# Graph product of a two-layer graph network: three pairs in seven block products, with h's blocks and sums kept in DRAM

## The chip, the cores and the metric

The kernel runs on one core of a Trainium2 chip. The metric is the device time of one execution in microseconds (us); the median of several runs is compared. All data is 32-bit float.

## The reference

For 16 batches of 1024 nodes with 256 channels there are two layers, each adding its result to x.

```python
# layer 0
h = relu(layernorm(x))
fea = h.transpose(0, 2, 1)                    # b, c, n
c = mean(fea, axis=1)                         # b, n: mean over the channels
A = abs(abs(sigmoid(c[:, None, :] - c[:, :, None]) - 0.5) - 0.5) * 2
g = relu(einsum('bcn,bnm->bcm', fea, adj * (A + A^T) / 2) * para)
q = g^T in 4 heads of 64;  k, v = h @ kv_w in 4 heads
x = x + softmax(q k^T * scale) v
# layer 1
h = relu(layernorm(x))
z = relu(batchnorm((A_hat h) @ W1.T + b1))    # A_hat: normalised adj + I, batchnorm over all rows
x = x + batchnorm(z @ W2.T + b2)
```

The change is in `einsum('bcn,bnm->bcm')`, here called the graph product: for each batch the transposed h (256 x 1024) times a weight matrix (1024 x 1024) that depends on the batch.

## The kernel before

The 1024 nodes of a batch are cut into NC = 8 blocks of 128 rows. The loop over b (lines 1306 onwards) does attention of batch b, then the graph product, values and keys of batch b+1, then the first linear stage of layer 1 for batch b (linear1_all). Batch 1 uses graph(), the later ones, 2 to 15, graph_seven(): 14 calls. After the loop, W2 and the batch norms follow; the change doesn't touch them.

Everything inside runs under a manual schedule: each engine (PE, ACT, DVE, POOL and SP, which issues transfers) executes its instructions in the order in which the program text issues them. Where a line stands decides what it queues behind on its own engine.

A weight block c (tile f_w, 128 x 1024) is made in two parts. `differences(b, c)` is two activations on ACT (lines 350 and 353), reading the row of sums f_row and writing the block. `masked(b, c)` is one instruction on DVE (line 358), which multiplies the block by the adjacency rows. The blocks live in the pool w4, which has five buffers; blocks 0 and 1 are made within the attention before.

In graph_seven the first PLAIN = 4 blocks are multiplied in the ordinary way: `plain(c)` issues 4 products of 128 x 128 by 128 x 512 (line 474). The other four blocks form two pairs. A pair is a 2 x 2 by 2 x 2 block product, and is done with seven products in place of eight (m1 to m_7, line 556), at the price of sums of blocks: t1 to t4 of the weights (lines 522 to 534, half-width subtractions on DVE) and s1 to s4 of h (lines 506 to 509). Three of the seven products add up in one PSUM bank x, from which ACT copies the partial results at three points (lines 589, 599, 604); m6 may write on only when the copy before it is done.

```python
            m1(0)
            m2(0)
            m1(1)
            nc.scalar.copy(room[:, 0], x)
            m_7(0)
```

`turn_h(b)` (line 362) puts h in transposed form into hT: two transposes of 32 x 32 blocks on DVE (line 369) into f_hQ, and 32 transfers on POOL's queue (line 376) from there into f_hT, both in SBUF. hT is wanted by `values` (line 447) and by the keys (line 636). Batch 0 does this on SP's queue.

`left` holds what remains of the attention: add0, collect (ACT), invert (four small DVE instructions, lines 762 to 765), spread (ACT, line 771), scale (DVE, line 780, and 16 transfers on SP's queue, line 797) and add1. graph_seven weaves these in. `partial` in the attention uses f_sums (lines 713 and 721); sums_h takes the same buffer afterwards.

linear1 calls three hooks, between[0] to between[2]. For batch b they prepare h of batch b+2: prepare_start (statistics), prepare_end (ReLU on ACT, line 279), and in linear1_seven prepare_row, which stores h's sums into frow (line 308) and loads them as f_row (line 309), both on SP's queue. linear1_seven makes its own sums on DVE (lines 987 to 991) and its products in line 995; line 1050 adds two of them. `load_thirds` loads six tiles of 512 KB (line 860) just ahead of graph_seven. These, hT and the attention's f_p share the eight buffers with the tag "p"; "acc" has two buffers.

Of the kernel before, what the change touches and what calls it, by code (L numbers as in the profile page):

```python
# [10 lines left out]
F32 = mybir.dt.float32  # L11
# [18 lines left out]
def fast_path(  # L30
# [143 lines left out]
    with ExitStack() as stage:  # L174
# [170 lines left out]
            differences(b, c)  # L345
            masked(b, c)

        def differences(b, c):
            w = w4.tile([P, N], F32, tag="w4", name=f"f_w_{b}_{c}")
            nc.scalar.activation(  # L350
                w, rows[b], AF.Abs, bias=cols[b][:, c : c + 1], scale=0.5 / C
            )
            nc.scalar.activation(w, w, AF.Tanh)  # L353
            ws[b, c] = w

        def masked(b, c):
            w = ws[b, c]
            nc.vector.scalar_tensor_tensor(w, w, 1.0, adj_t[c], ALU.subtract, ALU.mult)  # L358
# [3 lines left out]
        def turn_h(b, queue=nc.gpsimd):  # L362

            hTs[b] = []
            for d in range(CC):
                t = pp.tile([P, 4, NC, 32], F32, tag="acc", name=f"f_hQ_{b}_{d}", bufs=2)
                nc.vector.transpose(
                    t.rearrange("p k c r -> p c k r"),  # L370
                    hs[b][:, :, ts(d, P)].rearrange("p c (k i) -> p c k i", k=4),
                )
# [83 lines left out]
                )  # L456
            return copies

        PLAIN = 4

        def graph_seven(b, left, norm, last):

# [16 lines left out]
                            stop=(c == PLAIN - 1),  # L479
                        )  # L480

            turn_h(b)
            differences(b, 2)
            masked(b, 2)
            collect()
            invert()
            differences(b, 3)
            masked(b, 3)
            differences(b, 4)

            qT = big.tile([P, CC, N], F32, tag="qT", name=f"f_qT_{b}")
            nc.sync.dma_start(qT, para_v)
            spread()
            scale()
            masked(b, 4)
            plain(0)
            differences(b, 5)
            masked(b, 5)
# [3 lines left out]
            pairs_h = h[:, PLAIN:NC, :].rearrange("p (n k) c -> p n k c", k=2)  # L502
            a = lambda i, k: pairs_h[:, :, k, ts(i, P)]
            sums_h = ow.tile([P, 4, 2, P], F32, tag="sums", name=f"f_gs_{b}")
            s1, s2, s3, s4 = (sums_h[:, n] for n in range(4))
            nc.vector.tensor_sub(s3, a(0, 0), a(1, 0))
            nc.vector.tensor_add(s1, a(1, 0), a(1, 1))
            nc.vector.tensor_sub(s2, s1, a(0, 0))
            nc.vector.tensor_sub(s4, a(0, 1), s2)
            plain(1)  # L510
            differences(b, 6)
            masked(b, 6)

            def part_w(n, k, j):
                return ws[b, PLAIN + 2 * n + k][:, ts(j, 512)]

            t2 = [kT[:, n, 0:512] for n in range(2)]
            t3 = [kT[:, n, 512:N] for n in range(2)]
            t1, t4 = [None] * 2, [None] * 2

            def make_t3(n):
                nc.vector.tensor_sub(t3[n], part_w(n, 1, 1), part_w(n, 0, 1))

            def make_t1(n):
                t1[n] = part_w(n, 0, 1)
                nc.vector.tensor_sub(t1[n], t1[n], part_w(n, 0, 0))

            def make_t2(n):
                nc.vector.tensor_sub(t2[n], part_w(n, 1, 1), t1[n])
# [3 lines left out]
                t4[n] = part_w(n, 1, 0)  # L533
                nc.vector.tensor_sub(t4[n], t4[n], t2[n])

            make_t3(0)
            make_t1(0)
            plain(2)
            differences(b, 7)
            masked(b, 7)  # L540
            make_t2(0)
            plain(3)
            hT = hTs.pop(b)
            t23 = pp.tile([P, 2, 512], F32, tag="acc", name=f"f_kt23_{b}", bufs=2)
            rest = pp.tile([P, 2, 512], F32, tag="acc", name=f"f_kt4_{b}", bufs=2)
            sums = rest[:, 1].rearrange("p (n q) -> p n q", n=4)
            nc.sync.dma_start(sums, kvs_d)
            make_t3(1)
            make_t1(1)
            make_t2(1)  # L550
# [4 lines left out]
            def one(ps, left, right, n, more=True, fresh=False):  # L555
                nc.tensor.matmul(  # L556
                    ps,
                    left[:, n, :],
                    right,
                    start=fresh and n == 0,  # L560
                    stop=(n == 1),
                    skip_group_check=more,
                )

            def m1(n):
                one(x, a(0, 0), part_w(n, 0, 0), n, False, True)

            def m2(n):
                one(c_of[0, 0], a(0, 1), part_w(n, 1, 0), n)

            def m3(n):
                one(c_of[0, 1], s4, part_w(n, 1, 1), n)

            def m4(n):
                one(c_of[1, 0], a(1, 1), t4[n], n)

            def m5(n):
                one(x, s1, t1[n], n)

            def m6(n):  # L580
                one(x, s2, t2[n], n)

            def m_7(n):
                one(m7, s3, t3[n], n, False, True)

            m1(0)
            m2(0)
            m1(1)
            nc.scalar.copy(room[:, 0], x)
            m_7(0)  # L590
            m3(0)
            m2(1)
            make_t4(0)
            make_t4(1)
            m6(0)
            m_7(1)
            m3(1)
            m6(1)
            nc.scalar.copy(room[:, 2], x)
            m4(0)  # L600
            m4(1)
            m5(0)
            m5(1)
# [489 lines left out]
        def linear1_all(b, h1, thirds, early, late, last, ending=lambda: None, made=None):  # L1093
# [138 lines left out]
        with tc.manual_schedule(engines={ENG.PE, ENG.Activation, ENG.DVE, ENG.Pool, ENG.SP}):  # L1232
# [73 lines left out]
            for b in range(B):  # L1306
# [34 lines left out]
                    between[3].insert(0, roots_row)  # L1341
                    between[4] = scale[:3] + between[4] + [scale[3]]
                if b + 1 < B:
                    if 0 < b < B - 2:
                        thirds = load_thirds(b)
                    if b == 0:
                        qkv = graph(b + 1, between)
                        todo = []
                    else:
                        qkv, todo = graph_seven(b + 1, left, norm, b + 2 == B)  # L1350
                    if b == 0:
                        for step in scale[4:]:
                            step()
                        thirds = make_thirds(b)
                if b + 2 < B:
# [943 lines left out]
```

## Time and profile before

| | |
|---|---|
| median of 3 runs | 2403.58 us (2402.74 to 2403.99) |
| the profiled execution | 2403.7 us, of which the span is 2401.8 us |
| granted TensorE clock | 0.995 of full speed over the span |
| busy: PE, DVE, ACT, POOL | 98%, 80%, 56%, 13% of the span |
| plain graph products (line 474) | 448 records, 196.0 us together |
| weights: differences, masking | 147.0 and 134.3 us on ACT, 152.8 us on DVE, 127 blocks |
| hT transfers on POOL (line 376) | 480, 500 ns each |

PE is TensorE's matmuls, PEld its weight loads, DVE VectorE, ACT ScalarE, POOL GpSimd, SP the engine that issues most transfers; SPq is its queue. Busy time is the sum of an engine's instructions. One product in the source is two matmul records in the trace. In a line of a timeline the columns are start, length, engine, line of the kernel, operation, output <- input, shape and count; a bracket at the end gives the idle time before the instruction and what ended it.

### The profile page before, as it was taken

The page shows a single profiled execution, that of the slowest core. Times are in us where ns is not written, and L with a number is a line of the kernel's source. Part 1 is how long each engine was busy: PE and PEld are TensorE (multiplying, and loading weights), DVE is VectorE, ACT ScalarE, POOL GpSimd, SP SyncE. Part 2 cuts the span into 40 slices and gives each one's busy share as a digit, 9 for nine tenths or more (in the row PEclk, how much of TensorE's full clock was granted, in tenths as well). Part 3 has the DMA queues.
Part 4 walks back from the last instruction along what each step waited for, and adds up shares of the span by engine and source line. Part 5 has one row for each costly group of instructions (what it writes and reads, how often), then busy time and mean ns, then how long its engine had stood idle before and what let it go on. Part 6 is the DMA issues. An engine that isn't in the chain of part 4 may idle for free.

```text
span 2401.8 us, 24818 instructions
## 1 busy us (share of the span) xinstructions
PE 2364.5 (98%) x7978; PEld 1040.9 (43%) x7978; DVE 1920.9 (80%) x2694; ACT 1346.9 (56%) x1974; POOL 314.7 (13%) x561
## 2 busy tenths in 40 slices
PE   8999999999999999999999999999999999999996
PEld 4443444434343434444343434344443434444445
DVE  6787979696979788797969697887969698757766
ACT  6846555564646455555646465555556465446654
POOL 2030202011020302020210203020202011000000
PEclk9999999999999999999999999999999999999998
DMA  5042423332332414233323324142333122355579
GB/s 188 7 143 62 128 88 110 102 100 68 102 104 68 148 62 135 80 110 105 100 63 107 107 62 146 62 147 69 110 106 107 63 82 65 105 199 189 176 240 379
DMA packets 176411, 275.78 MB, mean 115 GB/s; under 512 B 37648, under 2 KB 121104, under 8 KB 176272
## 3 DMA queue, kind: packets, MB, share of 16 engines
q1 hardware_dynamic: 156112, 241.55, 31.3%
q0 software_dynamic: 15552, 15.77, 2.5%
q10 hardware_dynamic: 4608, 16.78, 1.7%
q8 instruction: 66, 1.08, 0.2%
q14 instruction: 73, 0.60, 0.1%
HBM read 169.35 MB, written 71.10 MB: 100 GB/s over the span
## 4 chain that ended last, share of the span: by engine, by line
PE 97%; DMA 1%; DVE 1%; issue 0%; ACT 0%; SPq 0%; DVEq 0%; ACTq 0%; POOLq 0%; POOL 0%
PE f_s L688 19%; PE f_o L729 19%; PE f_aps L889 16%; PE f_gps L474 8%; PE f_zps L995 6%; PE f_vps L447 4%; PE f_gps L556 4%; PE f_zx L1516 4%; PE f_zm L1516 3%; PE f_gpsx L556 3%; PE f_kpsx L636 2%; PE f_gps L401 2%; PE f_kps L636 1%; PE f_z2ps L1454 1%; PE f_outps L1739 1%; PE f_zps L1077 1%
## 5 line engine op out<-in xcount | busy, mean ns | idle before, releaser
L696 ACT ACTIVATE f_p<-f_s 128x1024 f32<-128x1024 f32 x512 | 477.3, 1046 | 149.1 <-PE f_s L688 149.1
L705 DVE TENSOR_TENSOR f_acc<-f_acc,f_p 128x1024 f32<-128x1024 f32 x384 | 470.5, 1225 | 41.8 <-DVE f_acc L705 1.4
L688 PE MATMUL f_s<-f_qT,f_kT 64*128 64x512 f32 x2048 | 457.1, 596 | 0.0
L729 PE MATMUL f_o<-f_p,f_v 128*64 128x512 f32 x2048 | 453.6, 595 | 0.0
L376 POOL DMA_DIRECT2D f_hT<-f_hQ x480 | 236.7, 500 | 1237.0 <-PE f_gps L474 1161.0
L688 PEld LDWEIGHTS f_s<-f_qT,f_kT 64*128 64x128 f32 x2048 | 190.3, 185 | 264.3 <-ACT f_p L696 118.4
L729 PEld LDWEIGHTS f_o<-f_p,f_v 128*64 128x64 f32 x2048 | 141.3, 137 | 304.4 <-issue 257.0
L474 PE MATMUL f_gps<-f_w,f_h_a 128*128 128x512 f32 x448 | 196.0, 595 | 0.0
L350 ACT ACTIVATE f_w<-f_row,f_col 128x1024 f32<-128x1024 f32 x127 | 147.0, 1158 | 29.6 <-DMA f_row<-frow 26.9
L358 DVE SCALAR_TENSOR_TENSOR f_w<-f_w,f_adj 128x1024 f32<-128x1024 f32 x127 | 152.8, 1213 | 3.8 <-ACT f_w L353 3.8
L353 ACT ACTIVATE f_w<-f_w 128x1024 f32<-128x1024 f32 x127 | 134.3, 1058 | 4.0
L474 PEld LDWEIGHTS f_gps<-f_w,f_h_a 128*128 128x128 f32 x448 | 84.0, 190 | 111.8 <-issue 99.1
L889 PE MATMUL f_aps<-f_ahatT,f_hs 128*128 128x512 f32 x256 | 115.1, 592 | 0.0
L889 PE MATMUL f_aps<-f_ahatT,f_h_b 128*128 128x512 f32 x256 | 113.4, 596 | 0.0
L447 PE MATMUL f_vps<-f_kvw,f_hT 128*128 128x256 f32 x512 | 113.1, 379 | 0.0
L889 PE MATMUL f_aps<-f_t,f_hs 128*128 128x512 f32 x256 | 112.5, 592 | 0.0
L279 ACT ACTIVATE f_h_b<-f_x,f_shift_b,f_rstd_b 128x256 f32<-128x256 f32 x128 | 66.3, 592 | 77.0 <-DVE f_shift_b L264 77.0
L447 PEld LDWEIGHTS f_vps<-f_kvw,f_hT 128*128 128x128 f32 x512 | 97.3, 190 | 20.1 <-issue 7.2
L279 ACT ACTIVATE f_h_a<-f_x,f_shift_a,f_rstd_a 128x256 f32<-128x256 f32 x126 | 73.8, 586 | 51.4 <-DVE f_shift_a L264 51.4
L702 DVE TENSOR_TENSOR f_acc<-f_p,f_p 128x1024 f32<-128x1024 f32 x64 | 76.3, 1192 | 14.8 <-ACT f_p L696 14.8
L756 ACT COPY f_parts<-f_red 32x64 f32<-32x64 f32 x128 | 39.0, 305 | 79.3 <-DVE f_red L721 78.1
L1018 ACT ACTIVATE f_z<-f_zps,f_b 128x512 f32<-128x512 f32 x60 | 38.0, 684 | 75.3 <-PE f_zps L995 75.3
(261 smaller groups left out, 3241.8 us busy)
## 6 DMA issues: line engine op xcount, KB each, us to landing
f_t<-ft SPq DMA_DIRECT2D x84, 512.0 KB, 7.0
fz<-f_z SPq DMA_DIRECT2D x64, 512.0 KB, 9.2
f_x<-in_x_dram SPq DMA_DIRECT2D x31, 1024.0 KB, 7.4
f_zb<-fz SPq DMA_DIRECT2D x42, 512.0 KB, 4.2
f_att<-f_oT SPq DMA_DIRECT2D x512, 32.0 KB, 1.9
fx<-f_x SPq DMA_DIRECT2D x16, 1024.0 KB, 4.4
f_hT<-f_hQ POOLq DMA_DIRECT2D x480, 32.0 KB, 2.8
f_qT<-in_L_gnn_para_dram SPq DMA_DIRECT2D x14, 1024.0 KB, 13.2
```

What stands on the lines that cost most here:

```text
L350: nc.scalar.activation(w, rows[b], AF.Abs, bias=cols[b][:, c : c + 1], scale=0.5 / C)
L358: nc.vector.scalar_tensor_tensor(w, w, 1.0, adj_t[c], ALU.subtract, ALU.mult)
L376: queue.dma_start(to[ts(k, 32), ts(a, 32 * NC)], t[ts(a, 32), k].rearrange("i c r -> i (c r)"),)
L447: nc.tensor.matmul(ps[:, i, :], hT[e][:, ts(c4 + i, P)], kvw_t[:, e, C : 2 * C], start=(e == 0), stop=(e == CC - 1),)
L474: nc.tensor.matmul(gps[d][:, ts(g, 512)], h[:, c, ts(d, P)], w[:, ts(g, 512)], start=(c == 0), stop=(c == PLAIN - 1),)
L556: nc.tensor.matmul(ps, left[:, n, :], right, start=fresh and n == 0, stop=(n == 1), skip_group_check=more,)
L688: nc.tensor.matmul(ps[:, e, :], kT[rows_e, pair, ts(m, P)], qT[rows_e, pair, ts(g, 512)], start=True, stop=True,)
L696: nc.scalar.activation(p, ps, AF.Exp)
L705: nc.vector.tensor_add(acc_of[s], acc_of[s], p)
L729: nc.tensor.matmul(o_of[s][e * HD : (e + 1) * HD, :], v[:, m, ts(2 * pair + e, HD)], p[:, e, :], start=(m == 0), stop=(m == NC - 1),)
L889: nc.tensor.matmul(ps, left[:, m, :], right(m), start=not more and m == 0, stop=(m == KH - 1), skip_group_check=more,)
L1516: nc.tensor.matmul(ps, left[:, m, :], right[:, m, :], start=start and m == 0, stop=(m == 1), skip_group_check=not start,)
```

## The change

PLAIN becomes 2, so that three pairs (blocks 2 to 7) go by seven products. The sums s1 to s4 of h are made by `pair_sums` during linear1_all, two batches ahead: for two pairs in its second hook, behind prepare_end, and for the third ahead of linear1_seven (the new hook `turning`), and are stored to DRAM (gs_d) by POOL. The transposes of h also move there (`turn_h_aside`), with 8 transfers on POOL's queue into hT_d in DRAM. graph_seven loads the sums, then hT, then para and the key sums on SP's queue, and only then the thirds (`load_more`). The order of graph_seven is new: blocks 2 to 4 are differenced first, block 7 lies in a buffer of the tag "acc", and m2 of the third pair stands between the first copy of x and the products that follow it.

```diff
+    hT_d = [dram.tile([CC, P, N], F32, tag=f"fhT_{b}", name=f"fhT_{b}") for b in range(B)]
+    gs_d = [dram.tile([P, 12, P], F32, tag=f"fgs_{b}", name=f"fgs_{b}") for b in range(B)]
...
-        PLAIN = 4
+        PLAIN = 2
+        PAIRS = (NC - PLAIN) // 2
...
+        def pair_sums(b, n0, n1):
+            n = n1 - n0
+            a = h_pairs(b, n0, n1)
+            t = pp.tile([P, 4, 2, P], F32, tag="p", name=f"f_gs_{b}_{n0}")
+            s1, s2, s3, s4 = (t[:, q, :n] for q in range(4))
+            nc.vector.tensor_sub(s3, a(0, 0), a(1, 0))
+            nc.vector.tensor_add(s1, a(1, 0), a(1, 1))
+            nc.vector.tensor_sub(s2, s1, a(0, 0))
+            nc.vector.tensor_sub(s4, a(0, 1), s2)
+            nc.gpsimd.dma_start(
+                gs_d[b][:, 4 * n0 : 4 * n1].rearrange("p (s n) q -> p s n q", s=4), t[:, :, :n]
+            )
+
+        def turn_h_aside(b):
+            for d in range(CC):
+                t = pp.tile([P, 4, NC, 32], F32, tag="p", name=f"f_hQ_{b}_{d}")
+                nc.vector.transpose(
+                    t.rearrange("p k c r -> p c k r"),
+                    hs[b][:, :, ts(d, P)].rearrange("p c (k i) -> p c k i", k=4),
+                )
+                to = hT_d[b][d].rearrange("(k i) n -> i k n", k=4)
+                for a in range(4):
+                    nc.gpsimd.dma_start(
+                        to[:, :, ts(a, 32 * NC)],
+                        t[ts(a, 32)].rearrange("i k c r -> i k (c r)"),
+                    )
...
-            turn_h(b)
+            w7 = pp.tile([P, N], F32, tag="acc", name=f"f_w_{b}_7", bufs=2)
+            rest = pp.tile([P, 2, 512], F32, tag="acc", name=f"f_kt4_{b}", bufs=2)
+            sums = rest[:, 1].rearrange("p (n q) -> p n q", n=4)
+            sums_h = ow.tile([P, 4, 2, P], F32, tag="sums", name=f"f_gs_{b}")
+            sums_c = rest[:, 0].rearrange("p (s q) -> p s q", s=4)
+            nc.sync.dma_start(sums_h, gs_d[b][:, 0:8].rearrange("p (s n) q -> p s n q", s=4))
+            nc.sync.dma_start(sums_c, gs_d[b][:, 8:12])
+            hT = []
+            for d in range(CC):
+                t = pp.tile([P, N], F32, tag="p", name=f"f_hT_{b}_{d}")
+                nc.sync.dma_start(t, hT_d[b][d])
+                hT.append(t)
+            qT = big.tile([P, CC, N], F32, tag="qT", name=f"f_qT_{b}")
+            nc.sync.dma_start(qT, para_v)
+            nc.sync.dma_start(sums, kvs_d)
+            load_more()
...
             differences(b, 2)
+            differences(b, 3)
+            differences(b, 4)
             masked(b, 2)
+            masked(b, 3)
             collect()
             invert()
...
             masked(b, 4)
             plain(0)
             differences(b, 5)
+            make_t3(0)
+            make_t1(0)
+            make_t2(0)
+            spread()
             masked(b, 5)
...
             plain(1)
             differences(b, 6)
+            differences(b, 7, w7)
+            m1(0)
+            m2(0)
+            make_t4(0)
+            m3(0)
+            m_7(0)
+            m1(1)
+            make_t3(1)
             masked(b, 6)
...
+            m2(1)
+            m4(0)
+            m_7(1)
+            m3(1)
             make_t1(1)
             make_t2(1)
...
+            scale()
+            masked(b, 7)
+            m1(2)
             nc.scalar.copy(room[:, 0], x)
...
+            make_t3(2)
+            make_t1(2)
+            make_t2(2)
+            m2(2)
+            m6(0)
+            m6(1)
             make_t4(1)
+            make_t4(2)
+            m_7(2)
+            m3(2)
+            m6(2)
             nc.scalar.copy(room[:, 2], x)
             m4(1)
+            m4(2)
+            for n in range(PAIRS):
+                m5(n)
+            t23 = pp.tile([P, 2, 512], F32, tag="acc", name=f"f_kt23_{b}", bufs=2)
             nc.scalar.copy(room[:, 1], x)
...
             def second(agg, up):
+                turning()
...
-                        thirds = load_thirds(b)
+                    def load_more():
+                        if 0 < b < B - 2:
+                            more_loads["thirds"] = load_thirds(b)
...
-                        lambda: prepare_end(b + 2),
+                        lambda: (prepare_end(b + 2), pair_sums(b + 2, 0, 2)),
                         lambda: (prepare_row(b + 2), again(b + 1)),
+                        turning=lambda: (pair_sums(b + 2, 2, 3), turn_h_aside(b + 2)),
```

More of the change, by code (lines that the diff above doesn't have):

```diff
@@ L346, in weights, with differences @@
             masked(b, c)
-        def differences(b, c):
-            w = w4.tile([P, N], F32, tag="w4", name=f"f_w_{b}_{c}")
+        def differences(b, c, w=None):
+            if w is None:
+                w = w4.tile([P, N], F32, tag="w4", name=f"f_w_{b}_{c}")
             nc.scalar.activation(
@@ L457, in values, with h_pairs, graph_seven @@
             return copies
-        PLAIN = 4
-        def graph_seven(b, left, norm, last):
+        PLAIN = 2
+        PAIRS = (NC - PLAIN) // 2
+        def h_pairs(b, n0, n1):
+            view = hs[b][:, PLAIN + 2 * n0 : PLAIN + 2 * n1, :].rearrange(
+                "p (n k) c -> p n k c", k=2
+            )
+            return lambda i, k: view[:, :, k, ts(i, P)]
+        def pair_sums(b, n0, n1):
[22 more added lines that the diff above has]
+                        t[ts(a, 32)].rearrange("i k c r -> i k (c r)"),
+                    )
+        def graph_seven(b, left, norm, load_more, last):
             gps = [ps_s.tile([P, N], F32, tag="s", name=f"f_gps_{b}_{d}") for d in range(CC)]
@@ L480, in plain @@
                         )
-            turn_h(b)
[L483 to L489, printed above, removed]
+            w7 = pp.tile([P, N], F32, tag="acc", name=f"f_w_{b}_7", bufs=2)
[10 more added lines that the diff above has]
+                hT.append(t)
             qT = big.tile([P, CC, N], F32, tag="qT", name=f"f_qT_{b}")
             nc.sync.dma_start(qT, para_v)
[L493 to L498, printed above, removed]
+            nc.sync.dma_start(sums, kvs_d)
+            load_more()
             kT = big.tile([P, CC, N], F32, tag="kT", name=f"f_kT_{b}")
@@ L501, in graph_seven, with s_of @@
             room = v.rearrange("p (n k) c -> p n (k c)", n=4)
[L502 to L512, printed above, removed]
+            a = h_pairs(b, 0, PAIRS)
+            def s_of(q):
+                return [sums_h[:, q, n] for n in range(2)] + [sums_c[:, q]]
+            s1, s2, s3, s4 = (s_of(q) for q in range(4))
             def part_w(n, k, j):
                 return ws[b, PLAIN + 2 * n + k][:, ts(j, 512)]
-            t2 = [kT[:, n, 0:512] for n in range(2)]
-            t3 = [kT[:, n, 512:N] for n in range(2)]
-            t1, t4 = [None] * 2, [None] * 2
+            t2 = [kT[:, n, 0:512] for n in range(2)] + [room[:, 3]]
+            t3 = [kT[:, n, 512:N] for n in range(2)] + [room[:, 1]]
+            t1, t4 = [None] * PAIRS, [None] * PAIRS
             def make_t3(n):
@@ L534, in make_t4 @@
                 nc.vector.tensor_sub(t4[n], t4[n], t2[n])
[L536 to L550, printed above, removed]
             x = ps_t.tile([P, 512], F32, tag="t", name=f"f_gpsx_{b}")
@@ L557, in one @@
                     ps,
-                    left[:, n, :],
+                    left,
                     right,
                     start=fresh and n == 0,
-                    stop=(n == 1),
+                    stop=(n == PAIRS - 1),
                     skip_group_check=more,
@@ L565, in m1 @@
             def m1(n):
-                one(x, a(0, 0), part_w(n, 0, 0), n, False, True)
+                one(x, a(0, 0)[:, n], part_w(n, 0, 0), n, False, True)
             def m2(n):
-                one(c_of[0, 0], a(0, 1), part_w(n, 1, 0), n)
+                one(c_of[0, 0], a(0, 1)[:, n], part_w(n, 1, 0), n)
             def m3(n):
-                one(c_of[0, 1], s4, part_w(n, 1, 1), n)
+                one(c_of[0, 1], s4[n], part_w(n, 1, 1), n)
             def m4(n):
-                one(c_of[1, 0], a(1, 1), t4[n], n)
+                one(c_of[1, 0], a(1, 1)[:, n], t4[n], n)
@@ L577, in m5 @@
             def m5(n):
-                one(x, s1, t1[n], n)
+                one(x, s1[n], t1[n], n)
             def m6(n):
-                one(x, s2, t2[n], n)
+                one(x, s2[n], t2[n], n)
             def m_7(n):
-                one(m7, s3, t3[n], n, False, True)
+                one(m7, s3[n], t3[n], n, False, True)
+            differences(b, 2)
+            differences(b, 3)
+            differences(b, 4)
+            masked(b, 2)
+            masked(b, 3)
+            collect()
@@ L586, in graph_seven @@
+            invert()
+            masked(b, 4)
+            plain(0)
+            differences(b, 5)
+            make_t3(0)
+            make_t1(0)
+            make_t2(0)
+            spread()
+            masked(b, 5)
+            plain(1)
+            differences(b, 6)
+            differences(b, 7, w7)
             m1(0)
             m2(0)
+            make_t4(0)
+            m3(0)
+            m_7(0)
             m1(1)
-            nc.scalar.copy(room[:, 0], x)
-            m_7(0)
-            m3(0)
+            make_t3(1)
@@ L592, in graph_seven @@
+            masked(b, 6)
             m2(1)
-            make_t4(0)
-            make_t4(1)
-            m6(0)
+            m4(0)
             m_7(1)
             m3(1)
-            m6(1)
+            make_t1(1)
+            make_t2(1)
+            scale()
+            masked(b, 7)
+            m1(2)
+            nc.scalar.copy(room[:, 0], x)
+            make_t3(2)
[3 more added lines that the diff above has]
+            m6(0)
+            m6(1)
+            make_t4(1)
+            make_t4(2)
@@ L599, in graph_seven @@
+            m_7(2)
+            m3(2)
+            m6(2)
             nc.scalar.copy(room[:, 2], x)
-            m4(0)
             m4(1)
-            m5(0)
-            m5(1)
+            m4(2)
+            for n in range(PAIRS):
+                m5(n)
+            t23 = pp.tile([P, 2, 512], F32, tag="acc", name=f"f_kt23_{b}", bufs=2)
             nc.scalar.copy(room[:, 1], x)
@@ L1091, in linear1_out, with linear1_all @@
                 nc.sync.dma_start(z1_d[t][:, f2 : f2 + 2, :], z)
-        def linear1_all(b, h1, thirds, early, late, last, ending=lambda: None, made=None):
+        def linear1_all(
+            b,
+            h1,
+            thirds,
+            early,
+            late,
+            last,
+            ending=lambda: None,
+            made=None,
+            turning=lambda: None,
+        ):
             sums = []
@@ L1343, in fast_path @@
                 if b + 1 < B:
-                    if 0 < b < B - 2:
-                        thirds = load_thirds(b)
+                    more_loads = {}
+                    def load_more():
+                        if 0 < b < B - 2:
+                            more_loads["thirds"] = load_thirds(b)
                     if b == 0:
@@ L1349, in fast_path @@
                     else:
-                        qkv, todo = graph_seven(b + 1, left, norm, b + 2 == B)
+                        qkv, todo = graph_seven(b + 1, left, norm, load_more, b + 2 == B)
+                        thirds = more_loads.get("thirds")
                     if b == 0:
```

## The prediction

> **What bounds the kernel now.** I read the page's engine shares first, then the chain of waits, then a table by stage of one batch (the one whose graph product begins at 520.45 us), then the timeline of PE, DVE, ACT and SP through that batch.
>
> ```profile
> PE 2364.5 (98%) x7978; PEld 1040.9 (43%) x7978; DVE 1920.9 (80%) x2694; ACT 1346.9 (56%) x1974; POOL 314.7 (13%) x561
> ...
> PE 97%; DMA 1%; DVE 1%; issue 0%; ACT 0%; SPq 0%; DVEq 0%; ACTq 0%; POOLq 0%; POOL 0%
> ```
>
> PE is busy 98% of the span and makes up 97% of the chain, so what counts is PE's own work and any new hole in it. Batches repeat every 131.67 us (PE starts the graph product at 388.78, 520.45, 652.12). The stage table has columns for PE, PEld, DVE, ACT, POOL, clock and DMA; its rows are the plain products, the seven products, the values and the keys:
>
> ```profile
> 520.45:534.29 13.84, 13.84 (x35) 6.19 (x33) 13.45 (x19) 12.06 (x18) 6.74 (x14) 1.00 0.95 323
> 534.29:546.30 12.01, 12.01 (x29) 5.32 (x28) 10.27 (x21) 1.90 (x3) 6.95 (x15) 1.00 0.52 120
> 546.30:553.21 6.91, 6.91 (x33) 6.08 (x32) 5.91 (x8) 2.29 (x5) 3.14 (x6) 1.00 0.11 29
> 553.21:559.58 6.37, 6.37 (x16) 2.27 (x14) 6.34 (x16) 4.80 (x7) 1.01 (x1) 1.00 0.49 165
> ```
>
> PE has no hole in these rows, but DVE is busy 13.45 of 13.84 us in the first: the second engine is nearly as full exactly where the change works. The timeline gives the paces (start, length, engine, line):
>
> ```profile
> 534.29 1.02 PE L556 MATMUL f_gpsx<-f_w,f_h_a 128*128 128x512 f32 x2
> 535.15 1.02 PE L556 MATMUL f_gps<-f_w,f_h_a 128*128 128x512 f32 x2
> ...
> 522.46 2.33 DVE L369 STREAM_TRANSPOSE f_hQ<-f_h_a 128x1024 f32<-128x1024 f32 x2
> ...
> 533.53 1.22 DVE L358 SCALAR_TENSOR_TENSOR f_w<-f_w,f_adj 128x1024 f32<-128x1024 f32 x1
> 534.67 0.69 DVE L522 TENSOR_TENSOR f_kT<-f_w,f_w 128x512 f32<-128x512 f32 x1
> 535.39 0.69 DVE L526 TENSOR_TENSOR f_w<-f_w 128x512 f32<-128x512 f32 x1
> 536.00 1.22 DVE L358 SCALAR_TENSOR_TENSOR f_w<-f_w,f_adj 128x1024 f32<-128x1024 f32 x1
> 537.13 0.68 DVE L529 TENSOR_TENSOR f_kT<-f_w,f_w 128x512 f32<-128x512 f32 x1
> ```
>
> One product of the source is two matmul records and goes by every 0.858 us. DVE starts this stage 2.01 us after PE (522.46 against 520.45): it has worked without a gap since L1050 at 460.37, so nothing in the attention lets it catch up further. Over the 14 batches that lag is 2.0 us in nine and 2.35 us in five. From start to start a masking (L358) takes 1.13 us, a half-width subtraction 0.61, or 0.72 if the next needs its result.
>
> **What the Trainium skill says.** "TensorE: Matmul & The Clock Gate", Architectural detail, says that PE's queue can pull weight loads ahead of running matmuls and that ACT and DVE are strict FIFO. The trace agrees: weight loads of 190 ns hide under matmuls, except behind a real wait. Here PE waits for a copy on ACT that ends at 423.30:
>
> ```profile
> 422.72 0.58 ACT L652 COPY f_kT<-f_kpsx 128x512 f32<-128x512 f32 x1
> ...
> 423.35 0.30 PEld L636 LDWEIGHTS f_kpsx<-f_kt,f_kt 128*128 128x128 f32 x2 [0.76 <-ACT f_kT L652]
> ```
>
> The load starts 0.05 us after the release, and the next product follows 0.96 instead of 0.86 us later (423.35 to 424.31): a stall costs its wait plus 0.10 us. The same page, Part 1, gives an idle window of about 3.4 us before the clock drops; the stalls below are shorter, and the table's clock is 1.00. "DMA: Bandwidth & Descriptors", Anatomy of one DMA, prices a transfer issued by POOL at 2.0 us plus bytes over 436 GB/s, 3.2 us for 512 KB; this trace has 4.2 us (fz to f_zb) to 7.0 us (six in a row). Its section on issuing engines says that all queues share the same 16 DMA engines; a rival rests on that.
>
> **The change part by part**, for each of the 14 batches that pass through graph_seven.
>
> 1. PE. Before: 4 plain blocks of 4 products and 2 pairs of 7, 30 products. After: 2 of 4 and 3 of 7, 29. One product less, 0.858 us; 14 x 0.858 = **12.0 us** if no hole opens.
>
> 2. DVE in this stage. Gone: two transposes (2.25) and four sums of h (1.59). Added: four half-width subtractions (2.7). The total falls by 1.1 us, but the deadlines come closer: plain products covered 13.8 us, now 6.9, and the last masked block, w7, formerly needed first at the second pair, must be ready at PE's 19th product. DVE's order to it from 522.46, by the paces above: masked 2, 3 (2.25), invert's four (1.28), masked 4 (1.13), make_t3, t1, t2 of pair 0 (2.05), masked 5 (1.13), make_t4(0) and t3(1) (1.22), masked 6 (1.13), t1(1), t2(1) (1.33), scale (1.14). masked(7) then starts at 535.12 and ends 1.21 later, **536.33**.
>
> 3. PE's clock to it: 534.29 was the 17th start; two products on, m2(2) could start at 534.29 + 1.72 = **536.01**. It waits to 536.38: 0.37, plus 0.10 to refill, 0.47 us; where DVE is 2.35 late, 0.82. Nine and five of them: 4.2 + 4.1 = **8.3 us given back**. All earlier meetings hold: w5 is ready at 530.4 for 531.7, t4(0) at 531.0 for 532.6, t3(1) at 531.6 for 533.4, w6 at 532.8 for 535.2. Later ones too: m6(0) needs the first copy, which ends about 536.8, and m2(2) runs beside it until 537.2; t3(2) is done at 537.1 for 539.0, t2(2) at 538.5 for 540.7, the two t4 by 539.7 for 541.6; m4(1), m4(2) cover the second copy.
>
> 4. ACT: the differences of blocks 3 and 4 move before collect, into the 4.8 us that ACT idled until f_red at 521.95 (they end at about 521.3): nothing. Blocks 6 and 7 follow plain(1) and end near 532, before DVE asks. If that idle time were absent, collect and all masks would come later.
>
> 5. SP: four more loads (sums twice, hT twice) at 0.35 to 0.55 us; kvs and the thirds move behind them. The first waits for the buffer that L721 frees at 521.91; behind it queue hT, qT, kvs, six thirds. Landing of the sums by the rows above: 522.4 + 4.2 to 7.0, so 526.6 to 529.4; m3(0) asks at 529.15. Cost 0 to 0.25 us; I take 0, as it goes first. All data is about 6 MB; at the first row's 323 GB/s it takes 19 us, to about 541; hT is asked at 545.9, the thirds 13 us after that. scale's 16 transfers go from 529.8 to 535.2, issue for 13.4 us, and land near 551; add1 wants them at 553.6. Nothing.
>
> 6. POOL: 32 transfers of 500 ns leave this stage; 10 come into the stage before. Each is dearer than those: 0.5 to 0.93 us (the latter the costliest small load, L81), 5 to 9 us of an idle engine. norm's rstd no longer queues behind them (it waited 2.2 us), off PE's path.
>
> 7. DVE in the stage before: 1.59 for two pair sums, at most as much for the third, 2.3 for the transposes. The first fall into the 5.32 us in which DVE waits for L941 (442.7 to 448.05); what follows delays L987 by 0.1 to 1.1 us: t3 at 454.6 for a product at 455.4, t4 at 456.8 for 458.9. DVE idles 1.69 us again before L1050. Cost 0; if that cover failed, DVE's lag would grow one for one.
>
> Sum: 12.0 - 8.3 = 3.7 us saved. The profiled execution took 2403.7 us (span 2401.8 and 1.9 around it), 0.1 above the median of 2403.58: **2399.9 us**. About 0.2% (4.8 us) is what a measurement of this kernel can tell from no change, so this case lies just inside.
>
> **The rivals.**
>
> (a) PE's hole closes: DVE passes masked(7) by 536.0, because the five late batches lose their 0.35 us or DVE is quicker than my paces. Then the full 12.0 us: **2391.6**. Half closed, 2395 to 2397. For it: the excess is only 0.37 us of a 14 us chain. Against: the paces repeat to 0.02 us from batch to batch, and DVE never waits in that chain.
>
> (b) Slower, by the row of sums. POOL's 1.75 MB of writes run at 448 to 462, and at 457.69 SP sends frow, whose small writes land only after 10 to 13 us; then comes f_row, and ACT waits:
>
> ```profile
> 474.06 1.15 ACT L350 ACTIVATE f_w<-f_row,f_col 128x1024 f32<-128x1024 f32 x1 [1.34 <-DMA f_row<-frow]
> ```
>
> ACT ends at 476.3, DVE wants the result at 478.26. Over the batches that slack is 0.7 to 2.1 us. Each microsecond beyond it delays DVE, which never recovers before the graph product, so PE stalls that much longer at w7. With row 3 us later: 3 - 1.35 = 1.65 us x 14 = 23 us more, 2399.9 + 23 = **2423**; 2 us later, 2409. It decides from about 2 us. Against: the two streams overlap by one or two transfers, which I estimate at 0.4 to 0.8 us.
>
> (c) Sums late: m3(0) stalls 0.25 to 0.85 us. Up to the 0.37 us it only moves the hole from w7; beyond, 0.5 x 14 = 7 us: 2400 to **2407**. That the work is not done as stated, so that PE issues 30 products, would be seen at L556; the diff leaves no room for it.
>
> **How the numbers follow.** The w7 hole as computed: 0.55, its own range 2396.5 to 2402.5; two fifths of it lie below 2398.8. Rival (a) 0.22, faster. (b) 0.15, slower. (c) and other small holes 0.08, mostly the same. Faster 0.55 x 0.4 + 0.22 = 0.44; slower 0.15 + 0.02 = 0.17; same 0.39. For 8 in 10 the range goes from the full gain, 2391, to the row 2 us late, 2409.
>
> **What would show it.** After: L474 has 224 records and L556 588; the time from the first plain product to the first value product falls from 25.85 to about 25.4 us. Right: one wait of PE before the product that reads w7, named after DVE's masking. Wrong: no such wait and 25.0 us (a); ACT waiting for f_row past 477 and DVE starting its maskings more than 2.4 us after PE (b); a wait for a DMA before m3(0) (c); or a hole in the keys or in L995, where I assume none.

## The result, and the profile after

| | before | after |
|---|---|---|
| median of 13 runs | 2402.9 us (2401.32 to 2403.99) | 2398.23 us (2396.7 to 2400.39) |
| profiled execution | 2403.7 us, span 2401.8 | 2398.78 us, span 2396.9 |
| from the first plain product to the first value product | 25.85 us | 25.45 us |
| start of one batch's graph product to the next | 131.67 us | 131.20 us, late batches about 131.57 |

The ratio is 0.998 with a 95% interval of 0.9971 to 0.9988: 4.7 us faster, where 3.7 were predicted. These are the page's lines for the engines, the chain of waits (shares of the span by engine) and the two groups of graph products (total and mean of one | idle time just before them and what ended most of it):

```profile
PE 2353.8 (98%) x7950; PEld 1032.4 (43%) x7950; DVE 1974.2 (82%) x2806; ACT 1346.8 (56%) x1974; POOL 174.1 (7%) x253
...
PE 72%; DVE 18%; ACT 4%; issue 3%; DMA 1%; SPq 1%; DVEq 0%; ACTq 0%; POOLq 0%; POOL 0%
...
L514 PE MATMUL f_gps<-f_w,f_h_a 128*128 128x512 f32 x224 | 99.9, 599 | 0.0
...
L576 PE MATMUL f_gps<-f_w,f_h_a 128*128 128x512 f32 x168 | 82.7, 601 | 3.8 <-DVE f_w L361 3.8
```

PE has 28 records less, which is one product (two records) less in each of 14 batches. PE's share of busy time is 98% as before. The chain, however, was 97% PE and now goes through DVE for 18%. A hole of half a microsecond is enough for that: the chain follows it back to what ended it, and from there through DVE's unbroken work into the attention. The chain says that two engines now set the end. It doesn't say how much the second one costs. That is read from the stage. Its table row (length, then PE, PEld, DVE, ACT, POOL, clock, DMA share, GB/s):

```profile
518.14:543.59 25.45, 25.26 (x60) 11.04 (x59) 22.51 (x37) 10.73 (x17) 0.81 (x1) 1.00 0.75 263
```

PE's busy time is now below the length of the stage. The timelines of PE, DVE and ACT show where; they hold m1 and m2 of the last pair, m6 of the first two pairs, scale, the masking of block 7, the first copy, and at the end m2(2) of a late batch (one in which DVE begins the stage 0.35 us later):

```profile
532.83 1.02 PE L576 MATMUL f_gpsx<-f_w,f_h_a 128*128 128x512 f32 x2
534.05 1.12 PE L576 MATMUL f_gps<-f_w,f_h_a 128*128 128x512 f32 x2 [0.19 <-DVE f_w L361]
535.01 1.88 PE L576 MATMUL f_gpsx<-f_kT,f_gs 128*128 128x512 f32 x4
...
531.64 1.22 DVE L835 TENSOR_TENSOR f_oT<-f_oT,f_recs 128x1024 f32<-128x1024 f32 x1
532.77 1.22 DVE L361 SCALAR_TENSOR_TENSOR f_w<-f_w,f_adj 128x1024 f32<-128x1024 f32 x1
...
533.89 0.58 ACT L641 COPY f_v<-f_gpsx 128x512 f32<-128x512 f32 x1 [4.21 <-PE f_gpsx L576]
...
665.62 1.13 PE L576 MATMUL f_gps<-f_w,f_h_a 128*128 128x512 f32 x2 [0.56 <-DVE f_w L361]
```

The masking ends at 532.77 + 1.22 = 533.99 and m2(2) starts at 534.05. Unhindered it would have started one pace after m1(2), at 532.83 + 0.858 = 533.69. It waits 0.36 us, and m6(0) follows 0.96 instead of 0.86 us later: 0.46 us lost. The bracket says 0.19 and not 0.36. The recorded end of a matmul is modelled (a product shows 1.02 us where the next starts after 0.858), so such a hole is measured from start to start. The bracket reads 0.17 to 0.20 us in eleven batches and 0.55 or 0.56 in three.

The two rows of the table differ: the stage is 0.40 us shorter and the batch 0.47. The rest, 0.06 to 0.07 us, is gained in the keys, where the third product waits for a copy on ACT. It starts 1.80 us after the first before, and 1.74 us after it in the changed kernel (first and third product of the keys, before and after):

```profile
553.21 1.02 PE L636 MATMUL f_kpsx<-f_hT,f_kvw 128*128 128x512 f32 x2
555.01 1.12 PE L636 MATMUL f_kpsx<-f_kt,f_kt 128*128 128x512 f32 x2
...
550.50 1.02 PE L691 MATMUL f_kpsx<-f_hT,f_kvw 128*128 128x512 f32 x2
552.24 1.12 PE L691 MATMUL f_kpsx<-f_kt,f_kt 128*128 128x512 f32 x2
```

Why this wait became shorter was not tried.

### The profile page after: what moved, and what is told of

The parts are those of the page before. It is cut to its first block, busy times and chain, and to the rows that moved or that the text cites. A ratio compares the mean times of both kernels' runs of the same rounds, so it can differ in the third digit from the quotient of the medians.

```text
span 2396.9 us, 24478 instructions
## 1 busy us (share of the span) xinstructions
PE 2353.8 (98%) x7950; PEld 1032.4 (43%) x7950; DVE 1974.2 (82%) x2806; ACT 1346.8 (56%) x1974; POOL 174.1 (7%) x253
## 3 DMA queue, kind: packets, MB, share of 16 engines
q8 instruction: 65, 1.06, 0.2%
## 4 chain that ended last, share of the span: by engine, by line
PE 72%; DVE 18%; ACT 4%; issue 3%; DMA 1%; SPq 1%; DVEq 0%; ACTq 0%; POOLq 0%; POOL 0%
PE f_aps L944 16%; PE f_s L743 12%; PE f_o L784 11%; PE f_zps L1050 6%; DVE f_acc L760 6%; PE f_vps L450 5%; PE f_zx L1588 4%; DVE f_w L361 4%; PE f_gpsx L576 3%; PE f_zm L1588 3%; ACT f_p L751 3%; PE f_gps L576 3%; PE f_kpsx L691 2%; PE f_gps L404 2%; PE f_kps L691 2%
## 5 line engine op out<-in xcount | busy, mean ns | idle before, releaser
L260 POOL TENSOR_TENSOR f_rstd_b<-f_var_b,f_mhalf 128x4 f32<-128x4 f32 (+1 forms) x31 | 33.1, 1069 | 1502.3 <-DVE f_var_b L259 1502.3
L514 PE MATMUL f_gps<-f_w,f_h_a 128*128 128x512 f32 x224 | 99.9, 599 | 0.0
L576 PE MATMUL f_gps<-f_w,f_h_a 128*128 128x512 f32 x168 | 82.7, 601 | 3.8 <-DVE f_w L361 3.8
L776 DVE TENSOR_REDUCE f_red<-f_sums 128x32 f32<-128x1024 f32 x64 | 78.1, 1220 | 2.2
## 6 DMA issues: line engine op xcount, KB each, us to landing
f_t<-ft SPq DMA_DIRECT2D x84, 512.0 KB, 10.9
```

The source lines that it names most:

```text
L576: nc.tensor.matmul(ps, left, right, start=fresh and n == 0, stop=(n == PAIRS - 1), skip_group_check=more,)
```

## The experiments

The theory: how much of the lost product's time is saved is fixed by one meeting, w7's masking on DVE against m2(2) on PE. DVE's position there decides, and nothing else in the new arrangement costs time. The rivals: m2(2) waits for something that only ends at the same moment; the gain comes from the new homes of the sums and transposes; or the DMAs share in it. The ratios are against runs of the kernel before beside the experiments, at 2403.18 us (the first four) and 2403.27 us (the others).

**scale behind the masking.** scale is the last DVE work ahead of masked(b, 7), and nothing on PE waits for it here.

```diff
             make_t2(1)
-            scale()
             masked(b, 7)
+            scale()
```

> One edit to the changed kernel: scale() (1.14 us on DVE, and its 16 transfers) stands behind masked(b, 7) instead of ahead of it. Theory (PE's hole ahead of the product that reads w7 is DVE's chain up to masked(7), 0.46 us in eleven batches and 0.81 in three): masking 7 comes 1.14 us earlier, the hole closes in all 14 batches, and 7.5 us go: 2398.2 - 7.5 = 2390.7 us, 0.995 of the kernel before. Rival A (the hole has another cause, such as the copy of x, the transfers or PE's own order): no change, 2398. Rival B (the transfers of scale, 1.1 us later, make add1 late): part of the gain is lost at the keys, 2393 to 2398.

Measured: 2392.09 us (2391.19 to 2392.42), ratio 0.9953 (0.9939 to 0.9966). From the timelines of PE and DVE, and its stage row:

```profile
532.78 1.02 PE L576 MATMUL f_gpsx<-f_w,f_h_a 128*128 128x512 f32 x2
533.64 1.02 PE L576 MATMUL f_gps<-f_w,f_h_a 128*128 128x512 f32 x2
534.50 1.96 PE L576 MATMUL f_gpsx<-f_kT,f_gs 128*128 128x512 f32 x4
...
531.59 1.22 DVE L361 SCALAR_TENSOR_TENSOR f_w<-f_w,f_adj 128x1024 f32<-128x1024 f32 x1
532.73 1.22 DVE L835 TENSOR_TENSOR f_oT<-f_oT,f_recs 128x1024 f32<-128x1024 f32 x1
```

```profile
518.09:543.16 25.07, 25.07 (x60) 11.04 (x59) 22.43 (x37) 10.72 (x17) 0.81 (x1) 1.00 0.75 267
```

m2(2) follows m1(2) after 0.86 us, and the list of PE's waits no longer has f_w of line 361. The batch now takes 130.82 us, 0.85 less than before. The chain of this kernel is 97% PE again. One line exchanged in DVE's order is worth 6.1 us on top of the change's 4.7, and add1, which wants scale's transfers, doesn't wait. This version beats both kernels. The expectation had 7.5 us. The stage shrinks by 0.38 us (25.45 to 25.07) and not by the 0.46 of the hole, because m6(0), unhindered by w7, now meets the first copy: its two products take 1.96 us instead of 1.88. So 0.78 of the batch's 0.85 us come from this stage and 0.07 from the keys.

**One more subtraction ahead of the masking.** make_t2(1) is issued twice, with the same result.

```diff
             make_t2(1)
+            make_t2(1)
             scale()
```

> One edit to the changed kernel: make_t2(1) is done twice, the second time with the same result, so that DVE has 0.72 us more ahead of masked(b, 7). Theory: the hole in PE grows one for one in every batch, 14 x 0.72 = 10.1 us: 2408.3 us, 1.002 of the kernel before. Rival A (the hole is not DVE's): 2398, as DVE's extra work lies beside PE's.

Measured: 2407.42 us (2406.12 to 2409.66), ratio 1.0018 (1.001 to 1.0025). From the view of waits (total, times, longest):

```profile
PE f_gps L576 <- DVE f_w L361: 13.1, 14, 1.3
```

In the changed kernel this wait had 3.8 us in 14. DVE later by one subtraction moves PE one for one: 9.3 us more wait, and 9.2 us more time than the changed kernel. The 10.1 us expected took the number of late batches as fixed; this trace has one late batch, not three. With the experiment before, DVE's arrival is moved to both sides, and the time follows both times.

**m2(2) behind the products that need the copy.**

```diff
             make_t2(2)
-            m2(2)
             m6(0)
             m6(1)
+            m2(2)
```

> One edit to the changed kernel: m2(2) stands behind m6(0) and m6(1) instead of ahead of them, so nothing runs beside the first copy of x. Theory: PE no longer waits for w7, but m6(0) now waits for the copy: PE ends m1(2) and the copy ends about 0.83 us later, plus 0.10 to refill, a hole of 0.93 us in all 14 batches in place of 0.46 (eleven) and 0.81 (three): + 11 x 0.47 + 3 x 0.12 = 5.5 us, 2403.7 us. The hole is then named after ACT. Rival A (PE runs on into the bank, or the copy is hidden): as much faster as the old hole, 2391.

Measured: 2404.11 us (2402.23 to 2405.53), ratio 1.0002 (0.9994 to 1.0011). From the view of waits, and from the timelines of PE and ACT:

```profile
PE f_gpsx L576 <- ACT f_v L641: 9.5, 14, 0.7
```

```profile
533.78 1.02 PE L576 MATMUL f_gpsx<-f_w,f_h_a 128*128 128x512 f32 x2
535.48 1.98 PE L576 MATMUL f_gpsx<-f_kT,f_gs 128*128 128x512 f32 x4 [0.68 <-ACT f_v L641]
...
534.84 0.59 ACT L641 COPY f_v<-f_gpsx 128x512 f32<-128x512 f32 x1 [4.21 <-PE f_gpsx L576]
```

Without another product beside the copy, m6(0) starts 1.70 us after m1(2): 0.84 us of wait and again 0.10 to refill, in all 14 batches. That is 0.94 x 14 = 13.2 us, more than the 12.0 us that the lost product brings. Seven products with three pairs are then worth nothing.

**Both together**, scale behind the masking and m2(2) behind m6 (the two edits above).

> Both edits: scale() behind masked(b, 7), and m2(2) behind m6(0) and m6(1). Theory: with the copy as the cause of the hole, DVE's earlier masking is worth nothing here: 2403.7 us, the same as with m2(2) moved alone within 1 us, and 13 us more than with scale moved alone. Rival (the hole is DVE's in every order): 2390.7, as with scale moved alone.

Measured: 2403.94 us (2403.37 to 2404.93), ratio 1.0004 (0.9995 to 1.0012), with the same wait for the copy, 9.5 us in 14. Here the earlier masking brings nothing, as m2(2) isn't what PE waits with. So the copy and the masking are two waits at one place: m2(2) beside the copy removes the first and runs into the second. With scale moved, m2(2)'s place beside the copy is worth 2403.94 - 2392.09 = 11.9 us.

**The moves alone.** PLAIN = 4 and two pairs, with products and weights in the order of the kernel before, 30 products, but with sums and transposes by way of DRAM. The third pair's sums are left out, as there is no third pair.

```diff
-        PLAIN = 2
+        PLAIN = 4
...
-                        turning=lambda: (pair_sums(b + 2, 2, 3), turn_h_aside(b + 2)),
+                        turning=lambda: turn_h_aside(b + 2),
```

> The moves alone: PLAIN stays 4, so two pairs and 30 products as in the kernel before and in nearly its order, but h's sums and transposes are made two hooks earlier, go through DRAM and are loaded first, as in the changed kernel. Theory (the saving is the one product less, and the moves cost and bring nothing, since PE had no hole in this stage before): 2403 us, 1.000 of the kernel before, within 2 us. Rival A (the moves themselves bring part of the gain, by the 32 transfers that leave POOL's queue): 2399 to 2401. Rival B (their DRAM traffic delays the row of sums or the thirds, and this takes part of the gain): 2405 or more.

Measured: 2402.97 us (2402.36 to 2404.2), ratio 0.9999 (0.9991 to 1.0007). The stage takes 25.85 us again, 361.96 us in all 14 batches as before, without a wait of PE. The moves by themselves bring nothing and cost nothing.

**The sums of h made in the stage**, by DVE at its head, and neither stored nor loaded.

```diff
-            nc.sync.dma_start(sums_h, gs_d[b][:, 0:8].rearrange("p (s n) q -> p s n q", s=4))
-            nc.sync.dma_start(sums_c, gs_d[b][:, 8:12])
+            sums_here(h_pairs(b, 0, 2), lambda q: sums_h[:, q])
+            sums_here(h_pairs(b, 2, 3), lambda q: sums_c[:, q : q + 1])
```

> The changed kernel with the move of h's sums undone: they are made by DVE at the head of the graph product (eight subtractions and additions, 1.6 us for two pairs and 1.05 for the third by the trace of the changed kernel) and are neither stored nor loaded; the transposes stay moved. Theory: DVE's chain begins 2.64 us later, and PE's holes grow by that and by 0.10 us for each further refill (two more): 14 x 2.85 = 40 us, 2438 us. Rival (what matters is the traffic through DRAM, and this saves 10.5 MB each way): 2398 or less.

Measured: 2434.54 us (2434.32 to 2434.75, 2 runs), ratio 1.0131 (1.0113 to 1.015). From its view of waits:

```profile
PE f_gps L583 <- DVE f_w L361: 26.9, 28, 1.4
...
PE f_gps L583 <- DVE f_kT L564: 6.4, 14, 0.8
```

36.3 us more than the changed kernel, 2.6 us a batch. The eight operations are 1.59 us for two pairs (the duration in the kernel before) and 1.06 us for the third (in the changed kernel), 2.65 us together. What DVE does more in this stage appears almost in full on PE, now at three meetings in place of one; the refills of the two further meetings, which the expectation of 40 us added, don't show in the time. So moving the sums is what makes the third pair pay, though the moves alone bring nothing. The move of the transposes, which takes another 2.25 us of DVE's work out of the stage, was not undone in any run; that it counts alike is argued, not shown.

**The thirds ahead of the sums** on SP's queue.

```diff
+            load_more()
             nc.sync.dma_start(sums_h, gs_d[b][:, 0:8].rearrange("p (s n) q -> p s n q", s=4))
...
             nc.sync.dma_start(sums, kvs_d)
-            load_more()
```

> The changed kernel with load_more() ahead of the loads of the sums, so that the six thirds (3 MB) go first on SP's queue; 13 of the 14 batches have them. Theory: the queue serves the sums after the thirds, at 323 GB/s some 9.7 us from 518.5, so that they land at about 530.5, while m3(0) asks at 526.8: a hole of 3.7 us that takes in the one at w7 (0.46), so 13 x 3.3 = 43 us more, 2441 us (2425 to 2455). PE's wait is then named after the transfer of the sums. Rival (the loads share the engines evenly, and the small one is through early): 2398 to 2405.

Measured: 2472.82 us (2472.59 to 2473.05, 2 runs), ratio 1.029 (1.0272 to 1.0309). The mechanism came, but the kernel is 74.6 us slower than the changed one, where 43 were expected. From the view of waits; the timelines of PE (m2(0), m3(0), m_7(0), m1(1)) and SP; and a table by stretches (length, PE, PEld, DVE, ACT, POOL, clock, DMA share, GB/s):

```profile
PE f_gps L576 <- DMA f_gs<-fgs: 49.5, 12, 5.1
```

```profile
538.60 1.02 PE L576 MATMUL f_gps<-f_w,f_h_a 128*128 128x512 f32 x2
543.35 1.86 PE L576 MATMUL f_gps<-f_w,f_gs 128*128 128x512 f32 x2 [3.73 <-DMA f_gs<-fgs]
545.01 1.91 PE L576 MATMUL f_gps<-f_kT,f_gs 128*128 128x512 f32 x2
546.71 1.18 PE L576 MATMUL f_gpsx<-f_w,f_h_a 128*128 128x512 f32 x2
...
530.29 3.33 SPq L915 DMA_DIRECT2D f_t<-ft  x6
533.71 0.39 SPq L529 DMA_DIRECT2D f_gs<-fgs  x1
```

```profile
539.46:543.35 3.89, 0.16 (x1) 0.00 (x1) 3.89 (x6) 2.82 (x3) 0.00 (x0) 1.00 1.02 412
543.60:547.01 3.41, 3.41 (x5) 1.35 (x5) 3.34 (x5) 0.00 (x0) 0.00 (x0) 0.50 1.02 409
```

The six thirds, 3 MB, fill the DMA engines, and the 512 KB of sums land after 9.3 us (median) in place of 3.6 us. The hole was expected at 3.7 us; in the 13 batches the bracket reads 3.35 to 5.10 us (the view names twelve after the DMA and one of 3.79 us, ahead of the same product, after DVE). What the expectation lacked is the second row: right after the hole the clock is at half, and the two products behind it pass every 1.66 and 1.70 us in place of 0.858. The trace has twelve such stretches from 267 to 1916 us, nine of 3.41 and three of 6.83 us, 51.2 us in all. PE works in 46.4 us of them, at half rate, so some 23.2 us are lost. The waits at line 576 (49.5 for the DMA and 4.0 for DVE, 3.8 in the changed kernel) rise by 49.7. The sum is 72.9 us, near the 2472.82 - 2398.23 = 74.6 us measured.

**Double the POOL stores.** The version with scale moved, and each of POOL's 8 stores of the transposes issued once more to a tensor in DRAM that nobody reads.

```diff
+                    for there in (to, hT2_d[b][d].rearrange("(k i) n -> i k n", k=4)):
+                        nc.gpsimd.dma_start(
+                            there[:, :, ts(a, 32 * NC)],
```

> The kernel with scale() behind masked(b, 7), with POOL's eight stores of the turned h issued twice, the second time to another DRAM tensor that nothing reads: 1 MB more written per batch in the stretch in which the row of sums is stored. Theory (the row has 0.7 to 2.1 us of slack, and the masking of block 7 now 0.7 us more): no change to 2392.1 us, within 1 us. Rival (POOL's writes delay the row of sums, and so DVE in the attention): each microsecond beyond the slack costs 14 us; 2395 to 2420.

Measured: 2390.89 us (2389.67 to 2392.38), ratio 0.9952 (0.9938 to 0.9966), against 2392.09 us without the second stores: 1.2 us below, in ranges that overlap, so no cost. The 14 stages take 351.1 us together in both. From the waits of ACT and of DVE:

```profile
ACT f_w L354 <- DMA f_row<-frow: 18.6, 11, 2.6
```

```profile
DVE f_w L362 <- ACT f_w L357: 3.8, 5, 1.1
```

ACT waits for the row 18.6 us in total, and 5.4 us without the doubled writes; the row's store lands after 12.7 us (median) instead of 10.0. That the writes are the cause isn't shown: the kernel before has none of them, and there the store takes 11.7 us and ACT waits 26.9 us. What is shown is that DVE's wait for the block stays at 3.8 us in 5, with the doubled writes, without them and in the kernel before. The slack in front of DVE takes all of ACT's longer waiting.

## Why the prediction was right, point by point

**PE (step 1)**: right. 14 products went, and with the hole closed the batch is 0.85 us shorter, where 0.858 was predicted; that the two agree so well is in part luck, as 0.07 of it comes from the keys. Rival (a), the full 12.0 us and 2391.6 us, is nearly what the kernel with scale moved does: 2392.09 us, 11.1 us below the kernel before. It was the right number for another order.

**DVE's chain and the meeting (steps 2 and 3)**: right in every place. Counted from PE's start of the stage, the masking of block 7 was predicted to start after 14.67 us and started after 14.63 (532.77 - 518.14); m2(2) was predicted after 15.93 and started after 15.91. The paces of single operations in the old profile, added up in the new order, gave the end of a chain that didn't exist yet to 0.04 us. The refill of 0.10 us, taken from a wait on a copy in another stage, returned here (0.96 in place of 0.86). The stage was to fall to about 25.4 us and is 25.45.

**The mis-sized term** is the count of late batches. The prediction took over five of 14, in which DVE begins 2.35 us after PE; there were three. So 11 x 0.46 + 3 x 0.81 = 7.5 us were given back, not 8.3, and 12.0 - 7.5 = 4.5 us were left. The traces confirm this sum: the 14 stages together take 361.96 us before and 357.47 after, 4.5 us less. What makes a batch late isn't settled: no experiment here was aimed at it, and the count differs from trace to trace (one with the further subtraction, four with two pairs).

That 4.5 comes so near to the measured 4.7 us, and to the 4.9 us between the two profiled spans, is in part luck. The gain in the keys, 14 x 0.07 = 1.0 us, stands in no step of the prediction. In the profiled execution it is hidden by the end of the kernel: from the first value product of the last batch to the last instruction it takes 408.9 us, before the change 406.7 us, though no graph product lies there. In the first four experiments' traces this stretch takes 407.0 to 409.4 us.

**ACT and SP (steps 4 and 5)**: no cost, as argued. The differences of block 4 end at 519.09, ahead of collect, which waits for f_red as before:

```profile
518.03 1.06 ACT L356 ACTIVATE f_w<-f_w 128x1024 f32<-128x1024 f32 x1
519.62 1.26 ACT L811 COPY f_parts<-f_red 32x64 f32<-32x64 f32 x4 [0.53 <-DVE f_red L776]
```

PE waits for no transfer in this stage; the sums are treated under rival (c).

**POOL and DVE in the stage before (steps 6 and 7)**: no cost, as argued, and cheaper than the bounds. The timelines of DVE (the first of the third pair's sums, the transposes, line 987 of the kernel before, the add ahead of which the delay ends) and of POOL:

```profile
447.06 0.28 DVE L478 TENSOR_TENSOR f_gs<-f_h_a 128x128 f32<-128x128 f32 x1
...
448.12 2.36 DVE L490 STREAM_TRANSPOSE f_hQ<-f_h_a 128x1024 f32<-128x1024 f32 x2
450.51 0.69 DVE L1042 TENSOR_TENSOR f_zt<-f_aggT 128x512 f32<-128x512 f32 x1
...
458.05 1.22 DVE L1105 TENSOR_TENSOR f_z<-f_z,f_zps 128x1024 f32<-128x1024 f32 x1 [2.05 <-ACT f_z L1073]
...
448.50 0.77 POOL L482 DMA_DIRECT2D fgs<-f_gs  x1 [2.15 <-DVE f_gs L481]
449.65 4.36 POOL L496 DMA_DIRECT2D fhT<-f_hQ  x8 [0.38 <-DVE f_hQ L490]
```

The third pair's four sums took 1.06 us (447.06 to 448.12) where up to 1.59 was allowed. The transposes' stores took 4.36 / 8 = 0.545 us each, and the sums' at most 0.77, where 0.5 to 0.93 was given. DVE still idles 2.05 us ahead of line 1105, so the delay ends there. That PE's stage is no longer than before with these moves alone is shown by the run with two pairs.

**The row of sums, rival (b)**: fell. The view of ACT's waits of the changed kernel has this line, where the kernel before had 26.9 us in 13:

```profile
ACT f_w L353 <- DMA f_row<-frow: 14.4, 12, 1.8
```

ACT waits less for the row, not 0.4 to 0.8 us a batch more, although POOL writes more beside it; why was not tried. In the run with doubled stores the row does come later, and the slack holds.

**The sums, rival (c)**: fell, by the place of the loads. SP and PE in the changed kernel:

```profile
519.62 0.33 SPq L528 DMA_DIRECT2D f_gs<-fgs  x1
...
522.65 5.45 SPq L915 DMA_DIRECT2D f_t<-ft  x6
...
526.83 1.02 PE L576 MATMUL f_gps<-f_w,f_gs 128*128 128x512 f32 x2
```

The sums go out at 519.62 and land 3.6 us later (median), about 523.2; m3(0) asks at 526.83. The prediction had taken 4.2 to 7.0 us, from loads on SP's queue; the 3.2 us that it works out beside them is for transfers issued by POOL, and POOL's store of 512 KB of sums lands after 3.0 us (median). The thirds, now behind everything, land after 10.9 us in place of 7.0 and nobody waits for them. With the thirds first, late sums do stop m3(0), for 3.35 to 5.10 us where the rival had at most 0.85, and with the clock's loss on top, which none of the predicted cases held, as none had a hole of that length.

## What to carry to other kernels

A product taken from an engine that is busy 98% is worth its time only if the second engine can follow: add up the second engine's paces to each block's first use before counting the gain, and look which of its operations ahead of the deadline nobody waits for. Here exchanging two such lines was worth 6.1 us where the product itself had brought 4.7. A PSUM copy that the next product waits for wants an independent product beside it (11.9 us here), and small loads with an early deadline belong ahead of large ones with a late deadline (74.6 us here).

## What the runs showed of the hardware that had not been expected

One hole too long costs twice. In the kernel with the thirds first the hole of 3.73 us is followed by 3.41 us at a clock of 0.50. This happens behind twelve of its 13 holes, and nowhere in the changed kernel from 230 to 2060 us. "TensorE: Matmul & The Clock Gate", Part 1: The HAM clock gate, gives an idle window of about 3.4 us and half rate after it. This case's trace agrees in the length and the rate, and adds that the window need not be all idle.

The twelve stretches begin on one grid of 3.413 us: 267.12, 407.07 and 543.60 us are 41 and 40 such steps apart, wherever PE's holes lie. What counts is what PE did in the grid step just ahead. The view by stretches of the same kernel has the step ahead of the drop at 820.08 us, and the two steps over which its shortest hole fell (3.35 us by the bracket, up to 1641.19 us):

```profile
816.67:820.08 3.41, 1.30 (x3) 0.68 (x4) 3.38 (x5) 0.97 (x1) 0.00 (x0) 1.00 1.03 414
1635.87:1639.28 3.41, 1.97 (x5) 0.57 (x3) 3.34 (x5) 3.09 (x4) 0.00 (x0) 1.00 1.00 395
1639.28:1642.70 3.42, 1.51 (x4) 0.79 (x5) 3.38 (x6) 1.22 (x2) 0.00 (x0) 1.00 1.04 419
```

A step with 1.30 us of PE's work was followed by half the clock, and steps with 1.51 and 1.97 us were not. Ahead of the other eleven drops PE worked 0 to 1.27 us. So it seems to be the place on the grid, and not the length alone, that decides whether a hole near 3.4 us costs more than itself; only one hole without a drop shows the other side. Holes up to 1.4 us (the run with the sums in the stage) left the clock at 1.00, and its 36.3 us are explained by DVE's work alone. The prediction had used that page only to set the loss aside.
